# Layer 3 of a four-layer image network: a second pass of one product, one small multiply on another engine, the joining's norms in steps, and its silus beside the chunk's own

## The chip, the cores and the metric

The kernel runs on one core of a Trainium2 chip, as one launch. The time is the device time of that launch in microseconds. The kernel before took 7278.3 us as the median of three runs (7276.84 to 7281.67).

## The reference, cut to what matters

Four layers run one after the other on x of 4 images x 64 channels x 128 x 128, float32. Only the last is touched. It is two selective scans over the same picture and a joining of their results:

```python
xc = silu(causal_conv(x @ in_w)); z = ...
dt, Bm, Cm = split(xc @ xproj_w)            # 16 states
dt = softplus(dt @ dt_w + dt_b)
h  = exp(dt * A) * h + dt * Bm * xc         # the scan, over the positions
y  = (sum over states of h * Cm + xc * D) * silu(z) @ out_w
...
spa = silu(group_norm(scan over all positions of all images)) + x
spe = silu(group_norm(scan over 8 tokens of 8 channels, for each pixel)) + x
w   = softmax(att_w)
out = spa * w[0] + spe * w[1] + x
```

The group norms have 4 groups per image, so neither scan's result can be joined before all of that image has been scanned: group_norm needs the mean and the variance over an image's pixels and 16 channels.

## The kernel before, in words

The network's first three layers end at about 3567 us of the span. Layer 3 works in 142 **chunks**, each of eight **steps**, one step for 16 of the 128 inner channels, with two scans for the halves of the 16 states: 65 chunks of the first scan ("spe", 64 pixels of 8 tokens, all four images side by side on the partitions), one short chunk ("run"), and 19 chunks for each of the four images of the second scan ("spa", 483 positions; the last of an image has 170). The constant ORDER = (0, 2, 4, 6, 1, 3, 5, 7) gives the order of the steps.

What a chunk does, by function and line:

- do_x: three matmuls, then ACT's two silus (xc L1416, zs L1417), then the load of the table set that holds exp and log (L1418).
- do_dt, in nine parts: softplus by relu, abs, exp and log on ACT (L1429 to L1437), summed on PE into a PSUM bank v, copied to dt by ACT (L1445, L1448). Part 8 is dtx = dt * xc: on DVE from v for spa (L1452), on POOL from dt for spe (L1454). dt and dtx are written to DRAM (do_put) and read back spread over partitions (do_copy), through SP's queue.
- do_bc and do_keep: the projections B and C, by PE into PSUM and by ACT into SBUF (L1465).
- for each step: do_exp, two exponentials dA on ACT (L1492) into PSUM; do_dB, dB = dtx * B, on DVE from PSUM (after do_sel on PE) for five of the eight steps (BY_DVE) and on POOL from SBUF for three (L1517); do_scan, two scans on DVE (L1524, L1529); do_hc, h * C on POOL (L1558, for spe two steps at a time).
- do_first, for spe only: the first token needs no scan. Its three parts are bb = B * C of token 0 (L1543), a matmul, and y0 (L1550, DVE).
- do_sums on PE, do_y on DVE (yz, L1600), the output's matmul, ACT copy and store (spa_out, spe_out), and do_stats, DVE's bn_stats (L1665), in every second spa chunk and four of them in every fourth spe chunk.

PSUM has two banks for the name "m", which v, the projections, the first part's matmul, the norms and the joining share, one for "y" and one for "dx". Four more hold dA.

When an image's last spa chunk is done, affine(b) makes the norms' scales and shifts of both scans for that image (L1744 to L1782, with norm_affine, L361 to L377): bn_aggr on DVE, two small matmuls, a square root on ACT and a reciprocal on DVE for each scan, and some twenty one-column or four-column operations on DVE. Then combine joins the image in eight groups of rows: loads (part 0), two silus on ACT with those scales and shifts (L1808, L1809; part 1), sums of three products on PE (parts 2 and 4) and copies by DVE (L1821; parts 3 and 5), and the store. One group goes beside each of the next image's first eight chunks; image 3's have none beside them.

The order of the work on PE, DVE, ACT and POOL is written by hand: scans() collects (8 * chunk + when, function) in a list, sorts it, and issues it in that order; "when" is in steps, so 8 is a chunk. Each engine takes its instructions in the order of this list, and waits at the first one whose data or buffer is not ready. The DMAs on SP's queue are issued by the same calls. In this list affine stands at 15.8 behind its image's last chunk, all of it in one entry. Group i of the joining has its silus at 10.37 + 8 * (i + 1); the do_x of a later chunk stands at 3.1 within a chunk's eight steps.

Of the kernel before, what the change touches and what calls it, by code (L numbers as in the profile page):

```python
# [9 lines left out]
F32 = mybir.dt.float32  # L10
BF16 = mybir.dt.bfloat16
AF = mybir.ActivationFunctionType
ALU = mybir.AluOpType
AX = mybir.AxisListType
# [3 lines left out]
NB, C, N = 4, 64, 128  # L18
# [6 lines left out]
ZC = 33  # L25
# [288 lines left out]
class Net:  # L314
# [1222 lines left out]
    def do_first(self, u, part):  # L1537

        nc = self.nc
        first = lambda t: t[..., 0::8]  # L1540
        if part == 0:
            u["bb"] = self.work.tile([128, 2, CPX], F32, name="bb", bufs=1)
            nc.gpsimd.tensor_tensor(u["bb"], first(u["BC"][0]), first(u["BC"][1]), ALU.mult)  # L1543
        elif part == 1:
            u["g"] = self.ps("m")[:, :CPX]
            for sg in range(2):
                self.mm(u["g"], self.c3["same"], u["bb"][:, sg], sg == 0, sg == 1)
        else:
            u["y0"] = self.work.tile([128, CPX], F32, name="y0", bufs=1)
            nc.vector.tensor_tensor(u["y0"], u["g"], first(u["dtx"]), ALU.mult)  # L1550
# [120 lines left out]
    def scans(self, us):  # L1671
        nc = self.nc
        self.turn, self.o1s = 0, {}
        chunks = GPX // CPX

        todo = []
        steps = [(u, q) for u in us for q in ORDER]
        by_pool = lambda j: ORDER[j % 8] not in BY_DVE
        for ci, u in enumerate(us):
            do = lambda when, f, *a: todo.append((8 * ci + when, len(todo), f, a))  # L1680
            spa = u["spa"]
            if spa:
                do(-22.0, self.spa_load, u)
            else:
                for part, when in enumerate((-2.9, 4.7, 6.42)):
                    do(when, self.do_first, u, part)
                m, i = divmod(u["at"], 4)
                do(-13.0, self.spe_taps, u)
                for g in range(8 if i == 0 else 0):

                    if m:
                        do(-48.0 + 3 * g if m > 1 else -48.0, self.spe_load, m, g)
                for g in range(8 if i == 3 or u["at"] == chunks - 1 else 0):
                    do(12.3 + 3 * g, self.spe_store, m, g)
            do(-12.9, self.do_x, u)
            for part, when in enumerate((-11.65, -11.25, -10.65, -10.05, -9.8, -9.55, -9.3, -9.0, -8.05)):
                do(when, self.do_dt, u, part)
            do(-7.7, self.do_put, u, "dt")
            do(-7.4, self.do_put, u, "dx")
            for k, when in enumerate((-9.07, -8.85, -7.24, -6.59)):  # L1700
                do(when, self.do_bc, u, k)
                do(when + 0.59, self.do_keep, u, k)
            for i, when in enumerate((4.7, 4.74, 5.9, 9.42, 9.74) if u["kind"] != "run" else ()):
                do(when, self.do_sums, u, i)
            if u["kind"] != "run":
                do(10.76, self.do_y, u)
                do(12.2, self.spa_out if spa else self.spe_out, u)
                do(13.64, self.do_stats, u)
        mine = [j for j in range(len(steps)) if not by_pool(j)]
        for j, (u, q) in enumerate(steps):  # L1710
            do = lambda when, f, *a: todo.append((j + when, len(todo), f, a))
            do(-6.0, self.do_copy, u, q, "dt")
            do(-1.56, self.do_exp, u, q, 0)
            do(-1.2, self.do_exp, u, q, 1)
            if by_pool(j):
                do(-6.5, self.do_copy, u, q, "dx")
                do(-4.22, self.do_dB, u, q, nc.gpsimd)
            else:
                do(-1.61, self.do_dB, u, q, nc.vector)
            do(0.1, self.do_scan, u, q, 0)  # L1720
            do(0.5, self.do_scan, u, q, 1)
            if u["kind"] == "run":
                do(0.55, self.keep_run, u, q)
            else:
                do(0.77, self.do_hc, u, q)
        for k, j in enumerate(mine):

            when = mine[k - 1] - 1.28 if k else -2.0
            todo.append((when, len(todo), self.do_sel, steps[j]))
        for ci, u in enumerate(us):  # L1730
            if u["kind"] == "spa" and u["at"][1] == SPC - 1:
                b = u["at"][0]
                do = lambda when, f, *a: todo.append((8 * ci + when, len(todo), f, a))
                do(15.8, self.affine, b)
                for i in range(8):

                    for part, when in enumerate((4.0, 10.37, 16.3, 16.75, 16.8, 17.51)):
                        do(when + 8 * (i + 1), self.combine, b, i, part)
        E = mybir.EngineType
        with self.tc.manual_schedule(engines={E.PE, E.DVE, E.Activation, E.Pool}):  # L1740
            for _, _, f, a in sorted(todo, key=lambda x: x[:2]):
                f(*a)

    def affine(self, b):  # L1744

        nc, c3, sm = self.nc, self.c3, self.small
        mv = sm.tile([128, 2], F32, name="mv0")
        nc.vector.bn_aggr(mv, self.st0.rearrange("p k s -> p (k s)"))
        s0, t0 = self.norm_affine(sm, mv, c3["gm16w"], c3["spa_gn_w"], c3["spa_gn_b"], self.eps)
        mv = sm.tile([128, 4, 2], F32, name="mv1")  # L1750
        for g in range(4):
            nc.vector.bn_aggr(mv[:, g, :], self.st1[:, g].rearrange("p k s -> p (k s)"))
        gm = c3["gme"][:, 128 * b : 128 * b + 128]
        four = lambda name: sm.tile([128, 4], F32, name=name)
        p = self.ps("m")
        self.mm(p[:, 0:4], gm, mv[:, :, 0])
        mean, q, rs = four("mean4"), four("q4"), four("rs4")
        nc.vector.tensor_copy(mean, p[:, 0:4])
        nc.vector.tensor_tensor(q, mv[:, :, 0], mean, ALU.subtract)
        nc.vector.tensor_tensor(q, q, q, ALU.mult)  # L1760
        nc.vector.tensor_tensor(q, q, mv[:, :, 1], ALU.add)
        p = self.ps("m")
        self.mm(p[:, 0:4], gm, q)
        nc.scalar.activation(rs, p[:, 0:4], AF.Sqrt, bias=self.eps)
        nc.vector.reciprocal(rs, rs)
        one = lambda name: sm.tile([128, 1], F32, name=name)
        s1, t1, m = one("s1"), one("t1"), one("m1")
        for of, to in ((rs, s1), (mean, m)):
            nc.vector.tensor_tensor(of, of, c3["goh"], ALU.mult)
            nc.vector.tensor_reduce(to, of, AX.X, ALU.add)  # L1770
        nc.vector.tensor_tensor(s1, s1, c3["spe_gn_w"], ALU.mult)
        nc.vector.tensor_tensor(m, m, s1, ALU.mult)
        nc.vector.tensor_tensor(t1, c3["spe_gn_b"], m, ALU.subtract)
        self.st = (s0, t0, s1, t1)

        k0, k1 = one("k0"), one("k1")
        nc.scalar.activation(k0, t0, AF.Silu)
        nc.scalar.activation(k1, t1, AF.Silu)
        nc.vector.tensor_tensor(k0, k0, c3["att"][:, 0:1], ALU.mult)
        nc.vector.scalar_tensor_tensor(k1, k1, c3["att"][:, 1:2], k0, ALU.mult, ALU.add)  # L1780
        for i in range(2):
            nc.vector.tensor_copy(self.parts(i)[3][:, :, ZC:96], k1.unsqueeze(2).to_broadcast([128, 8, 96 - ZC]))  # L1782

    def parts(self, i):

# [71 lines left out]
```

## Time and profile before

| | us |
|---|---|
| median of three runs | 7278.3 |
| the profiled execution | 7274.59 |
| its span | 7272.8 |
| PE busy, of the span | 6594.7 (91%) |
| DVE busy | 5372.9 (74%) |
| ACT busy | 4715.9 (65%) |
| POOL busy | 3438.8 (47%) |
| mean granted clock of TensorE | 0.952 |

The shares are of the whole span, and the four layers have different loads: PE's 91% are mostly of the first three, POOL's 47% almost all of the last. A share says little of layer 3; stretches of it do, and they are read by the answers to windows. In the groups of instructions each row has: line, engine, operation, tile written <- tiles read, size, count | busy time, mean ns of one | idle time of the engine just before, and what ended it. Busy time counts an instruction from its start to its end, and neighbours overlap a little: a scan of 1145 ns is followed by the next one some 1.11 us after its start.

### The profile page before, as it was taken

To read this page: it belongs to the slowest core of one execution; us is meant where nothing else is said; L and a number is where in the kernel's file an instruction comes from. 1 tells how busy PE (TensorE), PEld (TensorE's weight loads), DVE (VectorE), ACT (ScalarE), POOL (GpSimd) and SP (SyncE) were. 2 spreads that over 40 slices of the span, in tenths; PEclk is the share of its full clock that TensorE was granted. 3 is DMA by queue.
4 is the path that set the end of the run, shared out by engine and by line. 5 is a ranking of instruction groups with operands and counts; after the bars stand their busy time and mean duration, and the time that the engine had idled before them with its cause. 6 is when DMAs were issued, how large, how long until landed. Compare 5 with 4: busy or idle time off the path is not lost. (4 is left out here: it accounts for less than half of the span.)

```text
span 7272.8 us, 106459 instructions
## 1 busy us (share of the span) xinstructions
PE 6594.7 (91%) x39058; PEld 2862.1 (39%) x39058; DVE 5372.9 (74%) x7814; ACT 4715.9 (65%) x7768; POOL 3438.8 (47%) x1571
## 2 busy tenths in 40 slices
PE   8998999989999899988999999999888898898897
PEld 6335563347434563346533323333322332332333
DVE  3665546664565636654499999999999889899896
ACT  2564636653465536652487778777788788888885
POOL 1000000000000000000299999999899789789796
PEclk9998989989999989987999999999999999999998
DMA  3000110002000010002455555555455465554554
GB/s 91 1 1 1 29 47 1 1 1 74 2 1 1 28 47 1 1 1 84 146 149 152 150 151 152 151 151 148 135 159 150 133 175 146 143 170 141 155 165 122
DMA packets 364108, 647.01 MB, mean 89 GB/s; under 512 B 46784, under 2 KB 219584, under 8 KB 362048
## 3 DMA queue, kind: packets, MB, share of 16 engines
q1 hardware_dynamic: 357680, 609.91, 29.8%
q10 hardware_dynamic: 5904, 30.28, 1.2%
q8 instruction: 308, 5.05, 0.3%
q14 instruction: 216, 1.77, 0.1%
HBM read 517.80 MB, written 122.22 MB: 88 GB/s over the span
## 5 line engine op out<-in xcount | busy, mean ns | idle before, releaser
L1558 POOL TENSOR_TENSOR hc<-hd,C 128x910 f32<-128x910 f32 (+3 forms) x868 | 2314.1, 2680 | 250.3 <-DVE hd L1524 189.5
L754 DVE TENSOR_REDUCE nmz<-ps_sp 128x1 f32<-128x320 f32 x2048 | 895.3, 485 | 622.1 <-PE ps_sp L332 612.7
L770 ACT ACTIVATE big<-ps_sp 128x512 f32<-128x512 f32 (+1 forms) x1536 | 830.7, 592 | 719.0 <-PE ps_sp L332 717.7
L1524 DVE TENSOR_TENSOR_SCAN hd<-dA,hd 128x484 f32<-128x484 f32 (+1 forms) x1152 | 1235.3, 1109 | 72.5 <-ACT dA L1492 72.5
L1529 DVE TENSOR_TENSOR_SCAN hd<-dA,hd 128x512 f32<-128x512 f32 (+2 forms) x1120 | 1270.7, 1182 | 3.1 <-ACT dA L1492 3.0
L929 POOL TENSOR_TENSOR aw<-pack_a 128x128 f32<-128x128 f32 x8 | 3.5, 458 | 2185.4 <-PE ps_m L332 2185.4
L1517 POOL TENSOR_TENSOR hd<-s_dx,B 128x1024 f32<-128x1024 f32 (+5 forms) x450 | 960.2, 2135 | 12.0 <-DMA s_dx<-ddx 11.1
L332 PE MATMUL ps_dx<-dtx,c_sel 128*128 128x483 f32 (+3 forms) x1420 | 758.0, 616 | 218.4 <-DVE hd L1517 217.7
L332 PE MATMUL ps_sp<-uT,kT 32*128 32x512 f32 x3072 | 924.1, 649 | 1.4 <-ACT big L770 0.8
L1492 ACT ACTIVATE dA<-s_dt,c_spa_a 128x483 f32<-128x483 f32 (+3 forms) x1232 | 762.4, 640 | 158.1 <-DVE hd L1524 145.5
L1517 DVE TENSOR_TENSOR hd<-ps_dx,B 128x1024 f32<-128x1024 f32 (+5 forms) x750 | 808.4, 1080 | 73.7 <-PE ps_dx L332 72.6
L332 PE MATMUL ps_sp<-kT,qT 32*128 32x320 f32 x4096 | 817.3, 499 | 3.9 <-ACT qT L735 3.3
L1492 ACT ACTIVATE dA<-s_dt,c_spe_a 128x448 f32<-128x448 f32 x1040 | 636.3, 632 | 192.0 <-DVE hd L1529 190.9
L332 PE MATMUL ps_y<-hc,c_sum 128*32 128x455 f32 (+3 forms) x4512 | 603.9, 550 | 44.0 <-POOL hc L1558 44.0
L332 PE MATMUL ps_m<-sr,xht 128*128 128x483 f32 (+4 forms) x1136 | 509.4, 592 | 47.3 <-ACT sr L1436 47.3
L332 PEld LDWEIGHTS ps_dx<-dtx,c_sel 128*128 128x128 f32 x1420 | 225.8, 191 | 691.6 <-DVE hd L1517 289.5
L332 PEld LDWEIGHTS ps_sp<-uT,kT 32*128 32x128 f32 x3072 | 278.7, 185 | 437.5 <-issue 242.2
L332 PE MATMUL ps_o<-big,va 128*32 128x512 f32 (+1 forms) x3072 | 413.1, 610 | 0.0
L332 PE MATMUL ps_s<-pack_a,big 128*64 128x128 f32 (+4 forms) x2832 | 370.4, 305 | 43.5 <-DMA big<-in_x 19.8
L332 PEld LDWEIGHTS ps_sp<-kT,qT 32*128 32x128 f32 x4096 | 358.2, 190 | 57.2 <-issue 36.6
L332 PEld LDWEIGHTS ps_s<-pack_a,big 128*128 128x128 f32 (+2 forms) x2832 | 328.9, 179 | 65.3 <-issue 25.7
L332 PEld LDWEIGHTS ps_m<-sr,xht 128*128 128x128 f32 x1136 | 206.3, 193 | 348.2 <-issue 177.9
(396 smaller groups left out, 9585.7 us busy)
## 6 DMA issues: line engine op xcount, KB each, us to landing
s_dt<-ddt SPq DMA_DIRECT2D x520, 256.0 KB
s_dt<-ddt SPq DMA_DIRECT2D x544, 241.5 KB
s_dx<-ddx SPq DMA_DIRECT2D x195, 256.0 KB
s_dx<-ddx SPq DMA_DIRECT2D x204, 241.5 KB
ddt<-dt SPq DMA_DIRECT2D x65, 256.0 KB
ddx<-dtx SPq DMA_DIRECT2D x65, 256.0 KB
A<-x2s SPq DMA_DIRECT2D x136, 121.2 KB
ddt<-dt SPq DMA_DIRECT2D x68, 241.5 KB
```

Of the source, the lines that this page charges most:

```text
L332: self.nc.tensor.matmul(out, lhsT, rhs, start=start, stop=stop)
L754: nc.vector.tensor_reduce(self.nmz[n % 2][:, j, at : at + 1], p[:, :KEYS], AX.X, ALU.max, negate=True)
L770: nc.scalar.activation(slot(m, 2 * wu + q)[rows], p[rows], AF.Exp)
L929: nc.gpsimd.tensor_tensor(aw[i], k(f"aw{i + 1}"), k("sg"), ALU.mult)
L1492: self.nc.scalar.activation(t(u["dA", q][sg][:, at + u["lo"] : at + u["n"]]), t(u["dt", q]), AF.Exp, scale=a)
L1517: eng.tensor_tensor(v(dB[:, :, x:y]), v(d), v(u["BC"][0][:, :, x:y]), ALU.mult)
L1524: scan(hd[:, :m], dA[:, :m], hd[:, TOK : TOK + m], 0.0, ALU.mult, ALU.add)
L1529: scan(h[:, lo:n], dA[:, at + lo : at + n], dB[:, lo:n], init, ALU.mult, ALU.add)
L1558: mul = lambda to, a, b: self.nc.gpsimd.tensor_tensor(to, a, b, ALU.mult)
```

## The change

Four things are edited. (1) bb of the first scan's first token is computed by DVE in place of POOL. (2) The list of positions for do_dt gets a tenth entry, at -7.45 for the second scan and -8.05 for the first; do_dt itself is as before. The write of dtx to DRAM goes from -7.4 to -7.1 for the second scan. (3) affine is split. The first scan's norms of all four images are made once, in nine steps before image 0's last chunk (spe_affine); the second scan's are made per image, in nine steps (spa_affine) between 13.7 and 20.2. The root and the reciprocal become a log and an exponential of -0.5 times it on ACT, with one Newton step on DVE (rooted). (4) The joining's silus go from 10.37 to 11.095, which within eight steps is directly before the do_x at 3.1.

The diff; the removed body of affine is left out, since it is printed above.

```diff
--- before.py
+++ after.py
@@ -1540,7 +1540,7 @@
         first = lambda t: t[..., 0::8]
         if part == 0:
             u["bb"] = self.work.tile([128, 2, CPX], F32, name="bb", bufs=1)
-            nc.gpsimd.tensor_tensor(u["bb"], first(u["BC"][0]), first(u["BC"][1]), ALU.mult)
+            nc.vector.tensor_tensor(u["bb"], first(u["BC"][0]), first(u["BC"][1]), ALU.mult)
         elif part == 1:
             u["g"] = self.ps("m")[:, :CPX]
             for sg in range(2):
@@ -1693,10 +1693,10 @@
                 for g in range(8 if i == 3 or u["at"] == chunks - 1 else 0):
                     do(12.3 + 3 * g, self.spe_store, m, g)
             do(-12.9, self.do_x, u)
-            for part, when in enumerate((-11.65, -11.25, -10.65, -10.05, -9.8, -9.55, -9.3, -9.0, -8.05)):
+            for part, when in enumerate((-11.65, -11.25, -10.65, -10.05, -9.8, -9.55, -9.3, -9.0, -8.05, -7.45 if spa else -8.05)):
                 do(when, self.do_dt, u, part)
             do(-7.7, self.do_put, u, "dt")
-            do(-7.4, self.do_put, u, "dx")
+            do(-7.1 if spa else -7.4, self.do_put, u, "dx")
             for k, when in enumerate((-9.07, -8.85, -7.24, -6.59)):
                 do(when, self.do_bc, u, k)
                 do(when + 0.59, self.do_keep, u, k)
@@ -1731,55 +1731,115 @@
             if u["kind"] == "spa" and u["at"][1] == SPC - 1:
                 b = u["at"][0]
                 do = lambda when, f, *a: todo.append((8 * ci + when, len(todo), f, a))
-                do(15.8, self.affine, b)
+                for part, when in enumerate((13.7, 14.3, 15.1, 15.7, 16.55, 17.0, 18.0, 19.09, 20.2)):
+                    do(when, self.spa_affine, b, part)
+                for part, when in enumerate((-25.4, -23.4, -22.4, -20.4, -19.4, -18.0, -16.4, -12.91, -11.4) if b == 0 else ()):
+                    do(when, self.spe_affine, part)
                 for i in range(8):
 
-                    for part, when in enumerate((4.0, 10.37, 16.3, 16.75, 16.8, 17.51)):
+                    for part, when in enumerate((4.0, 11.095, 16.3, 16.75, 16.8, 17.51)):
                         do(when + 8 * (i + 1), self.combine, b, i, part)
         E = mybir.EngineType
         with self.tc.manual_schedule(engines={E.PE, E.DVE, E.Activation, E.Pool}):
             for _, _, f, a in sorted(todo, key=lambda x: x[:2]):
                 f(*a)
 
-    def affine(self, b):
...
+    def rooted(self, part, v, r, of=None):
+
+        nc = self.nc
+        if part == 0:
+            nc.vector.tensor_scalar(v, of, 1e-5, None, ALU.add)
+        elif part == 1:
+            nc.scalar.activation(r, v, AF.Ln)
+            nc.scalar.activation(r, r, AF.Exp, scale=-0.5)
+        else:
+            nc.vector.tensor_tensor(v, v, r, ALU.mult)
+            nc.vector.tensor_tensor(v, v, r, ALU.mult)
+            nc.vector.tensor_scalar(v, v, -0.5, 1.5, ALU.mult, ALU.add)
+            nc.vector.tensor_tensor(r, r, v, ALU.mult)
+
+    def spe_affine(self, part):
+
+        nc, c3, st = self.nc, self.c3, self.const
+        keep = lambda name, n: st.tile([128, n], F32, name="sa_" + name)
+        by_b = lambda t: t.rearrange("p (b g) -> p b g", b=NB)
+        each = lambda t: t.unsqueeze(1).to_broadcast([128, NB, 4])
+        if part == 0:
+            self.sa = a = dict(mean=keep("mean", 4 * NB), q=keep("q", 4 * NB), v=keep("v", 4 * NB), k=keep("k", NB))
+            for name in ("s", "t", "m"):
+                a[name] = keep(name, NB)
+            a["mv"] = mv = st.tile([128, 2, 4], F32, name="sa_mv")
+            for g in range(4):
+                nc.vector.bn_aggr(mv[:, :, g], self.st1[:, g].rearrange("p k s -> p (k s)"))
+            return
+        a = self.sa
+        if part in (1, 3):
+            a["p"] = p = self.ps("m")[:, : 4 * NB]
+            for b in range(NB):
+                of = a["mv"][:, 0] if part == 1 else a["q"][:, 4 * b : 4 * b + 4]
+                self.mm(p[:, 4 * b : 4 * b + 4], c3["gme"][:, 128 * b : 128 * b + 128], of)
+        elif part == 2:
+            mean, q = a["mean"], by_b(a["q"])
+            nc.vector.tensor_copy(mean, a["p"])
+            nc.vector.tensor_tensor(q, each(a["mv"][:, 0]), by_b(mean), ALU.subtract)
+            nc.vector.tensor_tensor(q, q, q, ALU.mult)
+            nc.vector.tensor_tensor(q, q, each(a["mv"][:, 1]), ALU.add)
+        elif part in (4, 5):
+            self.rooted(part - 4, a["v"], a["q"], a["p"])
+        elif part == 6:
+            self.rooted(2, a["v"], a["q"])
+            for of, to in (("q", "s"), ("mean", "m")):
+                v = by_b(a[of])
+                nc.vector.tensor_tensor(v, v, each(c3["goh"]), ALU.mult)
+                nc.vector.tensor_reduce(a[to], v, AX.X, ALU.add)
+            of = lambda w: w.to_broadcast([128, NB])
+            nc.vector.tensor_tensor(a["s"], a["s"], of(c3["spe_gn_w"]), ALU.mult)
+            nc.vector.tensor_tensor(a["m"], a["m"], a["s"], ALU.mult)
+            nc.vector.tensor_tensor(a["t"], of(c3["spe_gn_b"]), a["m"], ALU.subtract)
+        elif part == 7:
+            nc.scalar.activation(a["k"], a["t"], AF.Silu)
+        else:
+            nc.vector.tensor_scalar(a["k"], a["k"], c3["att"][:, 1:2], None, ALU.mult)
+
+    def spa_affine(self, b, part):
+
+        nc, c3 = self.nc, self.c3
+        one = lambda name: self.small.tile([128, 1], F32, name=name)
+        if part == 0:
+            self.fa = dict(mv=self.small.tile([128, 2], F32, name="mv0"))
+            nc.vector.bn_aggr(self.fa["mv"], self.st0.rearrange("p k s -> p (k s)"))
+            return
+        a = self.fa
+        mv = a["mv"]
+        if part in (1, 3):
+            a["p"] = self.ps("m")[:, 0:1]
+            self.mm(a["p"], c3["gm16w"], mv[:, 0:1] if part == 1 else a["q"])
+        elif part == 2:
+            a["mean"], a["q"] = one("gn_mean"), one("gn_q")
+            nc.vector.tensor_copy(a["mean"], a["p"])
+            nc.vector.tensor_tensor(a["q"], mv[:, 0:1], a["mean"], ALU.subtract)
+            nc.vector.scalar_tensor_tensor(a["q"], a["q"], a["q"], mv[:, 1:2], ALU.mult, ALU.add)
+        elif part == 4:
+            a["v"], a["s0"] = one("gn_v"), one("gn_s")
+            self.rooted(0, a["v"], a["s0"], a["p"])
+        elif part == 5:
+            self.rooted(1, a["v"], a["s0"])
+        elif part == 6:
+            s0, m, t0 = a["s0"], one("gn_ms"), one("gn_t")
+            a["t0"] = t0
+            self.rooted(2, a["v"], s0)
+            nc.vector.tensor_tensor(s0, s0, c3["spa_gn_w"], ALU.mult)
+            nc.vector.tensor_tensor(m, a["mean"], s0, ALU.mult)
+            nc.vector.tensor_tensor(t0, c3["spa_gn_b"], m, ALU.subtract)
+            self.st = (s0, t0, self.sa["s"][:, b : b + 1], self.sa["t"][:, b : b + 1])
+        elif part == 7:
+            a["k"] = one("k0")
+            nc.scalar.activation(a["k"], a["t0"], AF.Silu)
+        else:
+            k = a["k"]
+            nc.vector.scalar_tensor_tensor(k, k, c3["att"][:, 0:1], self.sa["k"][:, b : b + 1], ALU.mult, ALU.add)
+            for i in range(2):
+                nc.vector.tensor_copy(self.parts(i)[3][:, :, ZC:96], k.unsqueeze(2).to_broadcast([128, 8, 96 - ZC]))
 
     def parts(self, i):
```

More of the change, by code (lines that the diff above doesn't have):

```diff
@@ L1742, in scans @@
                 f(*a)
-    def affine(self, b):
[L1746 to L1782, printed above, removed]
```

## The prediction

> **What bounds the kernel now.** The page comes first. In its 40 slices, of 182 us each, only the last half changes: the diff touches layer 3, from about 3567 us.
>
> ```profile
> DVE  3665546664565636654499999999999889899896
> POOL 1000000000000000000299999999899789789796
> ```
>
> VectorE (DVE) and GpSimd (POOL) are both at nine tenths there, so which of them bounds a chunk must be read by stretch. One answer gives four: two chunks of the first scan (the first with the statistics), image 0's joining norms, and one chunk that carries a joining. The columns are stretch, length, then busy time of PE, weight loads, DVE, ACT, POOL, the granted clock, the DMA share and GB/s.
>
> ```profile
> 4512.00:4537.07 25.07, 22.90 (x89) 7.37 (x88) 25.07 (x27) 20.01 (x32) 24.59 (x10) 1.00 0.56 146
> 4537.10:4562.20 25.10, 23.42 (x90) 7.66 (x89) 24.40 (x24) 19.97 (x32) 25.10 (x10) 1.00 0.49 149
> 5732.86:5746.77 13.91, 3.89 (x12) 2.08 (x10) 7.26 (x29) 6.66 (x11) 4.71 (x3) 0.68 0.16 53
> 5790.30:5818.60 28.30, 25.33 (x92) 9.44 (x92) 25.01 (x29) 24.54 (x38) 23.52 (x12) 0.94 0.63 176
> ```
>
> A plain first-scan chunk is **POOL's**: 25.10 of 25.10. By the starts of the chunks' own silu (L1416), such chunks take 25.07 to 25.10, and every fourth, with four bn_stats, 25.56, all of it DVE's. A plain second-scan chunk, read the same way, takes 23.83 or 24.05 with DVE busy 23.4 or 24.0: it is **DVE's**. A joining chunk takes 28.0 to 28.7 with DVE busy 24.4 to 25.4: about 3.4 us are stalls. In the norms' 13.9 us no scan runs.
>
> **Part 1, first scan.** POOL's groups from 3650 to 5220 us:
>
> ```profile
> L1558 POOL TENSOR_TENSOR hc<-hd,C 128x1792 f32<-128x1792 f32 x250 | 1022.3, 4094 | 9.5 <-PE ps_dx L332 7.0 <-DVE dtx L1452 1.9 <-DVE hd L1529 0.5
> L1517 POOL TENSOR_TENSOR hd<-s_dx,B 128x1024 f32<-128x1024 f32 x187 | 446.9, 2390 | 0.0
> L1454 POOL TENSOR_TENSOR dtx<-dt,xc 128x512 f32<-128x512 f32 x62 | 79.7, 1285 | 0.0
> L1543 POOL TENSOR_TENSOR bb<-B,C 128x128 f32<-128x128 f32 x62 | 42.3, 682 | 0.0
> ```
>
> The work per chunk is 4 hc, 3 dB, one dtx, one bb, with no idle time. From start to start they take 4.07, 2.35, 1.24 and 0.64. The diff takes bb away. But its list for do_dt gains a tenth entry, and do_dt has only `else` behind part 7: the tenth entry computes **dtx a second time**. In the changed program's order POOL issues 130 dtx in place of 65, DVE 154 in place of 77. So POOL's sum rises by 1.24 - 0.64 = 0.60 in 49 chunks: 29.4 us. In the 16 chunks of 25.56 DVE decides: bb there costs it what y0, an op of its size, takes (255 ns busy), 0.2: 3.2. Together **+33**. bb's waits come under part 4.
>
> **Part 2, second scan.** DVE's groups behind 5237 us:
>
> ```profile
> L1452 DVE TENSOR_TENSOR dtx<-ps_m,xc 128x483 f32<-128x483 f32 x68 | 44.9, 661 | 47.1 <-ACT dt L1448 45.9
> L1669 DVE COPY hd<-hd 128x14 f32<-128x14 f32 x8 | 6.1, 765 | 0.3
> L363 DVE TENSOR_TENSOR gn_dv<-mv,gn_mean 128x1 f32<-128x1 f32 x4 | 3.0, 758 | 0.1
> ```
>
> A second dtx costs DVE 661 ns, 0.57 from start to start. Of 76 chunks 27 lie in the stretches of part 3; 49 x 0.57 = 28, less some 3 that DVE's idle time before the first dtx (0.41 per chunk) takes up in uneven chunks: **+25**. The write of dtx to DRAM goes 0.3 step (0.9 us) later, but POOL's first dB that needs it is over 4 steps (12 us) behind: nothing. The bank of v stays held to the second dtx, so later projections (do_bc) and, in joining chunks, the first sums wait on a chain through the one other bank. PE has 2.6 us free in a plain chunk (21.2 of 23.83): I take nothing.
>
> **Part 3, joining.** ACT's loads in the joining chunk at 5790 us:
>
> ```profile
> L1418 ACT ACT_TABLE_LOAD x1 | 1.3, 1283 | 0.0
> L1808 ACT ACT_TABLE_LOAD x1 | 1.3, 1283 | 0.0
> L1492 ACT ACT_TABLE_LOAD x1 | 1.3, 1283 | 0.0
> L1416 ACT ACT_TABLE_LOAD x1 | 1.3, 1283 | 0.0
> ...
> L1808 ACT ACTIVATE xht<-xht,gn_t,gn_s 128x552 f32<-128x552 f32 x1 | 0.8, 848 | 0.0
> L1809 ACT ACTIVATE xht<-xht,t,s 128x520 f32<-128x520 f32 x1 | 0.8, 806 | 0.0
> ```
>
> Two pairs of loads, one pair around each pair of silus. The diff puts the joining's silus directly before the chunk's own: one pair, 2.57 us of ACT less. What was two blocks of 4.2 and 3.8 us, in which no dA is made, is one of 5.4. DVE stalled 2.64 on dA and 0.7 before dtx. The one block, 1.6 longer than a plain chunk's, leaves about 0.8 of stall on dA (0.65 of slack in a plain chunk), and I add 0.4 each for the first sums and yz behind the held bank, plus the second dtx. Period 27.25 in place of 28.28: -1.03 x 24 (three images; the fourth joins in the tail) = -25. The norms go from one block into steps: 13.84 without a scan become 3.65 of DVE work: -10.2 x 3 = -31. Together **-55** (rounded). The low end: chunks at DVE's own 25.3, -47 more.
>
> By "ScalarE: Activation LUTs", What ACT_TABLE_LOAD costs, a switch also drains, 2.66 us in all, so that a pair saved would be 5.3. In the trace the next ACTIVATE starts 0.02 behind a load of 1283 ns; I stay with 2.57, and by the page the joining chunk would be at DVE's own work.
>
> **Part 4, waits for POOL.** The L363 row above has a mean of 758 ns for one column, and tile gn_mean's answer has 158/159/965 for it over 12. DVE and POOL side by side:
>
> ```profile
> 5736.43 0.16 DVE L361 COPY gn_mean<-ps_m 128x1 f32<-128x1 f32 x1 [3.16 <-PE ps_m L332]
> 5736.63 0.96 DVE L363 TENSOR_TENSOR gn_dv<-mv,gn_mean 128x1 f32<-128x1 f32 x1
> 5737.63 0.22 DVE L365 SCALAR_TENSOR_TENSOR gn_q<-gn_dv,mv 128x1 f32<-128x1 f32 x1
> ```
>
> ```profile
> 5733.32 2.09 POOL L1558 TENSOR_TENSOR hc<-hd,C 128x902 f32<-128x902 f32 x1
> 5735.37 2.21 POOL L1517 TENSOR_TENSOR hd<-s_dx,B 128x952 f32<-128x952 f32 x1
> ```
>
> The subtraction, both operands in SBUF, ends as POOL's op ends (5737.58). It does so in all three norms with POOL running, and takes 0.16 in the nine without. keep_run's copy (L1669), SBUF to SBUF, took 3.17 us beside an hc and 0.18 alone. The copy of a PSUM bank at 5736.43 took 0.16 beside the same POOL op. All scans, dB and dtx of DVE have an operand in PSUM; the diff's new steps mostly do not, and they stand among POOL ops of 2.1 to 2.2 us that fill 98% of a second-scan chunk.
>
> "SBUF — State Buffer", Who interferes with whom, states this rule: a DVE instruction with two SBUF operands and a POOL one exclude each other for a whole instruction, at most one does not. It speaks against this change; rows and rule agree, and the rule alone would leave the sum as it is.
>
> Price for one image's steps: q (2 ops), a Newton step with s, m, t (6 tensor_tensor), k with two copies (3). A first wait is on average half a POOL op, 1.1; each next op meets POOL's next op, 2.1, until POOL has used up its backlog, which at 5732.86 lasted 4.7 us. So 3.2 + 4.6 + 4 = 12, x 3 = **+36** (0, if all fall into gaps; 11 waits of 1.5, 50). The first scan's norms run once: 4 bn_aggr of 0.54 and 17 ops of 0.2, 5.6 of DVE's time in chunks that DVE bounds, and 10 of such waits: **+16** (6 to 20).
>
> bb has two SBUF operands as well. It is asked for 2.2 us after a scan; with the second dtx POOL is late enough that a dB (2.35) is then running, so that it waits some 1.4, inside DVE's slack of 25.70 - 24.40. I take nothing, and up to 1.3 in the 16 statistics chunks, +21, for the range.
>
> **Tail.** From image 3's bn_aggr (7208.6) to its first joining silu (7218.2) the norms are a chain of 9.6; without the first scan's part and the loads for roots it is about 5: **-5**.
>
> **Sum.** 33 + 25 - 55 + 36 + 16 - 5 = +50. The profiled execution took 7274.59 (span 7272.8), so 7325; the median of the runs, 7278.3, is 3.7 above it, hence 7328 as a median.
>
> **Rivals.** About 0.2% (14.6 us) is what a measurement of this kernel can tell from no change.
> - *No waits for POOL.* The strewn steps fall where POOL pauses, or hide in DVE's waits. Place: q, Newton, k. Price -46 to -52: 50 - 52 = -2, **7276**, not slower. It decides once waits fall under 37 in all. For it: POOL had 0.5 us free per chunk. Against it: three of three with POOL busy waited. 0.14.
> - *That, and joining chunks at DVE's own work.* -2 - 47 = -49: **7229**. For it: ACT is busy 24.5 of 28.3, less 2.6. Against it: the held bank. 0.08.
> - *bb misses POOL's gap.* If POOL starts its next op first, bb waits for a 4.07 hc: the chunk grows from 25.7 to about 28.7, 65 x 3 = 195: **7523**. Against it: the copy of 3.17 ended at POOL's boundary (5240.7), one sample. 0.10. If only in the statistics chunks, with the upper prices of part 4: 7345 to 7400. 0.18.
> - The forecast, 7293 to 7345: 0.50. *The change doesn't do what it says*: it does, and a second dtx more; the program's order is known.
>
> Faster 0.08, same 0.14, slower 0.78. The range goes from 7265 (most of "no waits") to 7400, and leaves out 0.08 below and 0.10 above.
>
> **What would show it.** L1454 x130 and L1452 x154; plain first-scan chunks at 25.7 with POOL full; plain second-scan chunks at 24.4 to 24.6; joining chunks near 27.2; one-column ops of the new steps with means near 1 to 2 us; bb's mean near 1.5. Wrong, if bb's mean is over 3, or the new steps' ops are at 0.16, or joining chunks come to 25.5.

## The result, and the profile after

The changed kernel takes 7529.7 us as the median of four runs (7526.65 to 7530.98), beside 7280.0 for the kernel before in the same job: ratio 1.0342, 95% interval 1.0325 to 1.036. It is **slower by 250 us**. The forecast was 7328 with a range up to 7400; the time is where the rival "bb misses POOL's gap" had put it, 7523, for a reason that this rival had only half, and in part by luck.

Where the time came in, by the starts of the chunks' silu in the two profiled executions (span 7272.8 before, 7529.2 after):

| stretch | before | after | difference | foreseen |
|---|---|---|---|---|
| layers 0 to 2, up to the first chunk | 3566.3 | 3581.7 | +15.4 | 0 |
| first scan, chunks 3 to 64 | 1562.8 | 1814.2 | +251.4 | +33 |
| second scan away from the joinings | 1095.2 | 1118.5 | +23.3 | +25 |
| chunks 82 and 83, which now hold the first scan's norms | 47.9 | 62.4 | +14.5 | +17, with two dtx |
| three stretches of norms and joining chunks | 795.1 | 751.8 | -43.3 | -19 |
| tail (image 3's norms and joining) | 139.9 | 133.3 | -6.6 | -5 |

(Chunks 0 to 2 add 1.7.) The first row isn't the change: those layers' instructions are the same, and over 14 profiled executions of kernels that differ only in layer 3 the first chunk begins between 3564.9 and 3584.8. Every row but the first scan's is within 25 us of what was foreseen; that one is 218 us above it.

In the page's slices POOL, at nine tenths in the first scan before, is at eight: it no longer bounds the stage. Windows of two first-scan chunks, a plain second-scan chunk and a joining chunk (length, then PE, weight loads, DVE, ACT, POOL, clock, DMA share, GB/s):

```profile
4615.10:4644.95 29.85, 26.14 (x89) 8.44 (x88) 27.45 (x25) 20.32 (x33) 26.76 (x10) 0.89 0.48 131
4644.95:4672.20 27.25, 23.50 (x89) 7.63 (x88) 26.51 (x25) 20.26 (x32) 24.19 (x10) 1.00 0.50 130
5636.90:5661.50 24.60, 21.35 (x76) 6.73 (x76) 24.54 (x26) 20.30 (x34) 23.38 (x12) 1.00 0.53 145
6102.50:6130.00 27.50, 24.02 (x93) 9.22 (x94) 25.14 (x29) 21.64 (x37) 23.49 (x12) 1.00 0.65 180
```

The first scan's chunk varies between 27 and 31, 29.26 on average over chunks 3 to 64, in place of 25.21. The granted clock does not explain it: the chunk at 1.00 is long too. The second scan's is 0.56 longer, the second dtx; the joining chunk is 0.8 shorter. The groups from 3650 to 5220 us say what POOL waits for, and what DVE does:

```profile
L1558 POOL TENSOR_TENSOR hc<-hd,C 128x1792 f32<-128x1792 f32 x216 | 882.3, 4085 | 178.8 <-DVE hd L1529 139.3 <-PE ps_dx L332 24.5 <-PE ps_m L332 15.0
L1454 POOL TENSOR_TENSOR dtx<-dt,xc 128x512 f32<-128x512 f32 x106 | 135.2, 1276 | 4.2
```

```profile
L1543 DVE TENSOR_TENSOR bb<-B,C 128x128 f32<-128x128 f32 x54 | 181.6, 3363 | 43.0 <-PE ps_m L332 43.0
```

Before, hc waited 9.5 us in this stretch, now 178.8, mostly for DVE's scans. And bb, 0.3 us of work on DVE, lasts 3.36 on average, behind 0.8 of idle time that ends with a product of PE. One chunk's timeline of DVE, of POOL and of PE (start, length, then what ran, and in brackets the idle time before with its releaser; the line ps_m<-bb is PE's read of bb, ps_m being one of the two "m" banks, here for g):

```profile
4528.29 2.31 DVE L1529 TENSOR_TENSOR_SCAN hd<-dA,hd 128x512 f32<-128x512 f32 x2
4531.34 3.57 DVE L1543 TENSOR_TENSOR bb<-B,C 128x128 f32<-128x128 f32 x1 [0.74 <-PE ps_m L332]
4534.83 1.22 DVE L1529 TENSOR_TENSOR_SCAN hd<-dA,hd 128x512 f32<-128x512 f32 x1
```

```profile
4528.27 2.35 POOL L1517 TENSOR_TENSOR hd<-s_dx,B 128x1024 f32<-128x1024 f32 x1
4530.59 4.07 POOL L1558 TENSOR_TENSOR hc<-hd,C 128x1792 f32<-128x1792 f32 x1
4534.63 2.51 POOL L1517 TENSOR_TENSOR hd<-s_dx,B 128x1024 f32<-128x1024 f32 x1
```

```profile
4530.65 0.66 PE L332 MATMUL ps_m<-bb,c_same 128*128 128x64 f32 x4
```

DVE's scans end at 4530.60. bb has one buffer, and PE reads the previous chunk's bb until 4531.3, so bb can't start. By then POOL's hc has run for 0.75 us, and bb, with both operands in SBUF, ends just behind it (4534.91 and 4534.66). It is so in every chunk but the first: 64 of the 65 bb start inside an hc and end 0.24 to 0.26 behind its end. The first, at 3597.02, meets no operation of POOL and takes 0.39: two operands in SBUF alone do not make it slow. Had bb been ready at 4530.60, it would have stood at the boundary between dB and hc.

### The profile page after: what moved, and what is told of

The parts are those of the page before. It is cut to its first block, busy times and chain, and to the rows that moved or that the text cites. A ratio compares the mean times of both kernels' runs of the same rounds, so it can differ in the third digit from the quotient of the medians.

```text
span 7529.2 us, 106476 instructions
## 1 busy us (share of the span) xinstructions
PE 6668.4 (89%) x39058; PEld 2870.4 (38%) x39058; DVE 5646.1 (75%) x7925; ACT 4654.2 (62%) x7709; POOL 3492.2 (46%) x1571
## 5 line engine op out<-in xcount | busy, mean ns | idle before, releaser
L332 PE MATMUL ps_dx<-dtx,c_sel 128*128 128x483 f32 (+3 forms) x1420 | 790.8, 640 | 337.6 <-DVE hd L1517 333.0
L1492 ACT ACTIVATE dA<-s_dt,c_spa_a 128x483 f32<-128x483 f32 (+3 forms) x1232 | 759.4, 640 | 178.8 <-DVE hd L1524 160.9
L332 PE MATMUL ps_y<-hc,c_sum 128*32 128x455 f32 (+3 forms) x4512 | 639.4, 581 | 97.3 <-POOL hc L1558 97.3
L332 PE MATMUL ps_m<-sr,xht 128*128 128x483 f32 (+4 forms) x1136 | 524.6, 605 | 60.5 <-ACT sr L1436 60.5
```

What stands on the lines that cost most here:

```text
L332: self.nc.tensor.matmul(out, lhsT, rhs, start=start, stop=stop)
L1492: self.nc.scalar.activation(t(u["dA", q][sg][:, at + u["lo"] : at + u["n"]]), t(u["dt", q]), AF.Exp, scale=a)
```

## The experiments

Two theories were set against each other. **Port** (the "lock theory" of the expectations): bb on DVE waits because both of its operands are in SBUF while POOL's hc runs; where in POOL's work it falls sets the price. **Queue or dtx:** the second dtx on POOL, or bb's place in DVE's order and its wait for PE, makes the chunk long by itself. The kernel before was run beside them in each job: 7284.5, 7284.3, 7280.8 and 7283.8.

**bb back on POOL**, the second dtx kept:

```diff
-            nc.vector.tensor_tensor(u["bb"], first(u["BC"][0]), first(u["BC"][1]), ALU.mult)
+            nc.gpsimd.tensor_tensor(u["bb"], first(u["BC"][0]), first(u["BC"][1]), ALU.mult)
```

> The changed kernel with bb back on POOL; the second dtx stays. Lock theory (bb on DVE, both operands in SBUF, waits to the end of POOL's hc and so makes the first-scan chunk 29.2): the wait is gone, POOL bounds the chunk with 4 hc, 3 dB, 2 dtx and bb, 25.1 + 1.24 = 26.3 to 26.4 us, and the time falls by 62 x 2.8 = 175 to about 7355. Rival (POOL's second dtx makes the chunk long): the chunk stays near 29 and the time near 7520.

Measured: 7374.9 (7373.4 to 7376.7), chunk 26.93. The direction is the port theory's, -155, but the chunk isn't always POOL's 26.3: 25 of the 62 take 27.7 to 28.1, with DVE waiting for the product for dB (132.1 us of idle time before dB between 3650 and 5220 us). More on that below.

**One dtx**, bb left on DVE:

```diff
-            for part, when in enumerate((-11.65, -11.25, -10.65, -10.05, -9.8, -9.55, -9.3, -9.0, -8.05, -7.45 if spa else -8.05)):
+            for part, when in enumerate((-11.65, -11.25, -10.65, -10.05, -9.8, -9.55, -9.3, -9.0, -8.05)):
-            do(-7.1 if spa else -7.4, self.do_put, u, "dx")
+            do(-7.4, self.do_put, u, "dx")
```

> The changed kernel with dtx computed once, as before the change; bb stays on DVE. Lock theory: bb still meets an hc, the first-scan chunk stays between 27.5 and 29.2, and only the second scan's chunks give back 0.56 each (76 of them, 40 us): 7400 to 7490. Rival (the second dtx is what lengthens the first-scan chunk): it falls to 25.0 and the time to about 7225.

Measured: 7395.8 (7392.9 to 7404.0), just under the range; chunk 27.93, bb's mean 2.37. The second dtx isn't the main part of the chunk's length: without it the chunk falls by 1.3 only, and bb still falls into an hc, only later in it.

**Both undone**: the edits of the last two together.

> The changed kernel with dtx computed once and bb on POOL: only the split norms and the joined silus are left. Both theories: first-scan chunk as before (25.07), joining chunks 27.3 - 0.56 = 26.8 in place of 28.3 (24 x -1.5 = -36), norms about -10 each (-30), the first scan's norms +13, tail -5: 7280 - 58 = about 7222. A second rival (the new steps of the norms cost what the old block did): 7245 or more.

Measured: 7219.9 (7203.6 to 7223.6), ratio 0.9906 (0.9892 to 0.9921). What is left of the change, the norms in steps and the joined silus, is **worth 65 us**. Against this kernel bb on DVE alone costs 176, the second dtx alone 155, both together 310.

**One operand of bb in PSUM**: PE copies C's first tokens into the free part of the bank that holds the previous chunk's g; everything else as in the changed kernel.

```diff
-            nc.vector.tensor_tensor(u["bb"], first(u["BC"][0]), first(u["BC"][1]), ALU.mult)
+            tok = self.g_at[:, CPX : 3 * CPX] if self.g_at is not None else self.ps("m")[:, CPX : 3 * CPX]
+            tok = tok.rearrange("p (s x) -> p s x", s=2)
+            self.mm(tok, self.c3["id"], first(u["BC"][1]))
+            nc.vector.tensor_tensor(u["bb"], first(u["BC"][0]), tok, ALU.mult)
         elif part == 1:
-            u["g"] = self.ps("m")[:, :CPX]
+            self.g_at = self.ps("m")
+            u["g"] = self.g_at[:, :CPX]
...
```

> The changed kernel, bb on DVE, but its second operand is first copied by PE into the unused part of the PSUM bank that holds the previous chunk's g, so that DVE reads only one operand from SBUF; the second dtx stays, and PE does one 128-column product more per chunk. Lock theory: bb takes about 0.3 and the chunk falls to 25.7 to 26.0 (POOL's two dtx, no bb): about 7310. Rival (what costs is bb's place in DVE's queue and its wait for PE, not the operands' place): bb and the chunk stay as they are, 7500 or more.

Measured: 7640.6 (7637.5 to 7648.2), a miss. From 3650 to 5220 us:

```profile
L1546 DVE TENSOR_TENSOR bb<-B,ps_m 128x128 f32<-128x128 f32 x50 | 19.3, 386 | 275.5 <-PE ps_m L332 275.5
```

bb itself is 0.39 each time (in 61 chunks beside a running dB of POOL); but DVE waits 5.5 us for the copy, which stands in PE's queue behind sums that wait for an hc. The edit had made a new wait in place of the old one. Mended, with the copy directly behind the previous chunk's g and bb one scan later:

```diff
+            nc.vector.tensor_tensor(u["bb"], first(u["BC"][0]), u["tok"], ALU.mult)
+        elif part == 3:
+            bank = self.g_at if self.g_at is not None else self.ps("m")
+            u["tok"] = bank[:, CPX : 3 * CPX].rearrange("p (s x) -> p s x", s=2)
+            self.mm(u["tok"], self.c3["id"], first(u["BC"][1]))
...
-                for part, when in enumerate((-2.9, 4.7, 6.42)):
+                do(-3.29, self.do_first, u, 3)
+                for part, when in enumerate((-2.45, 4.7, 6.42)):
```

> The changed kernel with bb on DVE and one of its operands in PSUM, as in the run before of that kind, but PE's copy stands directly behind the previous chunk's g and bb one scan later, so that DVE doesn't wait for the copy; the second dtx stays. Lock theory: bb takes 0.39 without any wait for POOL, the first-scan chunk falls from 29.2 to about 26 (POOL's two dtx), and the time to about 7325. Rival (an op more on DVE at this place costs 3 us whatever its operands): 7500 or more.

Measured: 7346.4 (7342.2 to 7350.4), chunk 26.42.

```profile
L1543 DVE TENSOR_TENSOR bb<-B,ps_m 128x128 f32<-128x128 f32 x59 | 21.1, 358 | 0.0
```

```profile
4124.48 0.36 DVE L1543 TENSOR_TENSOR bb<-B,ps_m 128x128 f32<-128x128 f32 x1
```

```profile
4121.54 4.09 POOL L1563 TENSOR_TENSOR hc<-hd,C 128x1792 f32<-128x1792 f32 x1
```

The same multiplication on the same engine, at 0.36 (0.35 to 0.40 over all 65) where it was 3.36. It stands later in the order now, but 63 of the 65 still start inside an hc, mostly with 1.1 us or more of it to go, and don't wait for its end: that both operands are in SBUF is what makes bb wait.

**Two buffers for bb**, on the changed kernel:

```diff
-            u["bb"] = self.work.tile([128, 2, CPX], F32, name="bb", bufs=1)
+            u["bb"] = self.work.tile([128, 2, CPX], F32, name="bb", bufs=2)
```

> The changed kernel with two buffers for bb in place of one, so that bb doesn't wait for PE's read of the previous chunk's bb (0.8 us per chunk in the changed kernel). Lock theory: bb is asked for 0.8 earlier, while the same hc of POOL already runs or just starts, and ends when that hc ends: bb's median grows from 3.6 to about 4.2, the chunk stays near 29 and the time within 15 of 7530. Rival (the wait for PE makes bb miss the gap between POOL's ops): bb comes before the hc, its median falls under 1 and the time to about 7320.

Measured: 7403.9 (7398.5 to 7405.8), bb's median 0.72, its mean from 3650 to 5220 us 0.70. Here the expectation from the port theory **fell**, and the rival was right on bb, though not on the time (7320): one more buffer of 512 bytes per partition takes away 126 us. bb then is asked for while a dB runs (in 63 of the 65 chunks), waits a few tenths for its end, and goes ahead of the hc, which is 4.26 in place of 4.08:

```profile
4140.02 0.72 DVE L1543 TENSOR_TENSOR bb<-B,C 128x128 f32<-128x128 f32 x1
```

```profile
4138.13 2.36 POOL L1517 TENSOR_TENSOR hd<-s_dx,B 128x1024 f32<-128x1024 f32 x1
4140.44 4.26 POOL L1558 TENSOR_TENSOR hc<-hd,C 128x1792 f32<-128x1792 f32 x1
```

So the wait for the port was real, but that it was the wait for an *hc* came from the buffer.

That left open whether the buffer alone decides. **One dtx, two buffers**, on the kernel of the run shown next (7202.5), which has one dtx, bb on POOL and the first scan's norms elsewhere:

```diff
-            u["bb"] = self.work.tile([128, 2, CPX], F32, name="bb", bufs=1)
-            nc.gpsimd.tensor_tensor(u["bb"], first(u["BC"][0]), first(u["BC"][1]), ALU.mult)
+            u["bb"] = self.work.tile([128, 2, CPX], F32, name="bb", bufs=2)
+            nc.vector.tensor_tensor(u["bb"], first(u["BC"][0]), first(u["BC"][1]), ALU.mult)
```

> The kernel with one dtx and the norms in the idle chunks (7202), with one edit: bb on DVE with two buffers. The run with two buffers and two dtx showed bb meeting the end of a dB (0.7) in place of an hc (3.6). Theory that POOL's lag decides where bb falls: without the second dtx POOL is earlier, bb meets an hc just begun, DVE waits 2 to 4 us, the first-scan chunk is 27 or more and the time about 7320 to 7400. Rival (the wait for PE's read alone decided): bb falls into a dB as with two dtx, POOL's chunk loses bb's 0.64, the chunk is 24.5 to 25.0 and the time about 7180 to 7200.

Measured: 7382.6 (7378.2 to 7383.3), chunk 27.92. DVE and POOL in one chunk:

```profile
4121.07 3.40 DVE L1543 TENSOR_TENSOR bb<-B,C 128x128 f32<-128x128 f32 x1
```

```profile
4120.13 4.09 POOL L1558 TENSOR_TENSOR hc<-hd,C 128x1792 f32<-128x1792 f32 x1
4124.17 2.53 POOL L1517 TENSOR_TENSOR hd<-s_dx,B 128x1024 f32<-128x1024 f32 x1
```

No wait for PE any more, and bb still waits 3: without the second dtx POOL is earlier, and the hc began 0.94 before bb. Both conditions are needed: bb early enough, and POOL late enough.

**The first scan's norms in the idle chunks**, on the kernel with both undone:

```diff
-                for part, when in enumerate((-25.4, -23.4, -22.4, -20.4, -19.4, -18.0, -16.4, -12.91, -11.4) if b == 0 else ()):
+                for part, when in enumerate((-146.0, -145.4, -144.8, -144.2, -143.6, -142.8, -141.8, -140.91, -139.5) if b == 0 else ()):
```

> One dtx and bb on POOL, and the first scan's norms moved from beside image 0's last full chunks to the chunks just behind the first scan, where POOL is busy 10 us of 24. If the price of these steps (two chunks of 62.6 in place of 47.9) is DVE's waits for POOL and its full queue there: those two chunks go back to 24 each and the steps cost 0 to 4 at their new place, 7220 - 13 = about 7207. Rival (the steps cost their chain of PE, ACT and DVE wherever they stand): 7220.

Measured: 7202.5 (7197.3 to 7206.4), ratio 0.9887 (0.9872 to 0.9902): the fastest of all, 82 us under the kernel before in its job. Chunks 82 and 83 are back at 47.9, and chunk 67 grew by 5.8, so the move is worth some 9 by the chunks' starts; the rest of the 17 between the two medians lies within the spread of the runs.

**The silus apart again**, on the kernel with both undone:

```diff
-                    for part, when in enumerate((4.0, 11.095, 16.3, 16.75, 16.8, 17.51)):
+                    for part, when in enumerate((4.0, 10.37, 16.3, 16.75, 16.8, 17.51)):
```

> One dtx and bb on POOL, and the joining's silus back at 10.37, away from the chunk's own: only the norms in steps are left of the change. If the joined silus make the joining chunk 26.2 in place of 28.3: 24 x 2.1 = 50 come back, 7220 + 50 = about 7270. Rival (the steps of the norms brought most of the gain): 7235 or less.

Measured: 7263.5 (7255.4 to 7270.3), joining chunks back at 28.36 on average of seven for each image. So the joined silus are worth 44 of the 65, and the norms in steps, with the first scan's at their bad place, the other 21.

**bb on DVE with a PSUM operand and one dtx**, on the kernel with the norms in the idle chunks; the copy and bb's place are as in the mended run:

```diff
-            nc.gpsimd.tensor_tensor(u["bb"], first(u["BC"][0]), first(u["BC"][1]), ALU.mult)
+            nc.vector.tensor_tensor(u["bb"], first(u["BC"][0]), u["tok"], ALU.mult)
```

> The kernel with one dtx and the norms in the idle chunks (7202), with one edit: bb on DVE with one operand copied to PSUM by PE. Lock theory: bb takes 0.36 wherever it falls, POOL's chunk loses 0.64, DVE's 24.4 gains 0.3: plain chunks 24.7, those with bn_stats 25.9, so 49 x -0.35 + 16 x 0.3 = -12, about 7190. Rival (PE's copy and the held bank cost the first-scan chunk what the move gains): 7202 or more.

Measured: 7213.5 (7207.5 to 7215.2), 11 more than 7202.5. bb takes 0.37, in 61 chunks beside a running dB of POOL, and POOL has its 0.64 less (24.4), yet a plain chunk stays at 25.07, with 0.4 of DVE's time waiting for the product for dB, and one with statistics grows to 25.87. Moving bb to DVE in this form doesn't pay even without its waits; why DVE waits there is open.

**The rest of the second dtx.** With bb's wait gone the chunk was 26.42 or, with two buffers, 27.31, and POOL's work is 25.7. DVE, in the run with two buffers, waits for the product for dB (114.5 us from 3650 to 5220 us) as in the run with bb on POOL; PE and DVE there:

```profile
4144.76 1.22 PE L332 MATMUL ps_y<-hc,c_sum 128*32 128x448 f32 x4 [2.22 <-POOL hc L1558]
4145.91 2.08 PE L332 MATMUL ps_dx<-dtx,c_sel 128*128 128x512 f32 x2
```

```profile
4148.02 1.22 DVE L1517 TENSOR_TENSOR hd<-ps_dx,B 128x1024 f32<-128x1024 f32 x1 [2.78 <-PE ps_dx L332]
```

POOL, late by the second dtx, gives hc late; PE stands at the sum over it, and the product for DVE's dB is queued behind that sum. PE has little room to catch up: contrary to what was said of its 91% ahead of the prediction, it is about as busy in layer 3 as before it (3275 us from 3567 us on, 3320 up to there), and 22.9 to 23.4 of a first-scan chunk's 25.1. The edit puts the sum behind the product:

```diff
-            for i, when in enumerate((4.7, 4.74, 5.9, 9.42, 9.74) if u["kind"] != "run" else ()):
+            for i, when in enumerate((4.7, 5.8 if not spa else 4.74, 5.9, 9.42, 9.74) if u["kind"] != "run" else ()):
```

> The changed kernel with two buffers for bb (7404), with one edit: PE's first sums over hc in a first-scan chunk go from 4.74 to 5.8, behind the product for dB at 5.72. If what is left of the chunk's length (27.3 where POOL's work is 25.7) is PE standing at sums whose hc POOL has not finished, so that the product for DVE's dB behind them comes late: the chunk falls to 25.8 to 26.3 and the time by 62 x 1.2 to about 7330. Rival (POOL's second dtx delays DVE's scans by another way, through its own dB or dt): no change, 7404.

Measured on the kernel with two buffers: 7382.1 (7366.9 to 7409.6), inconclusive: in chunks 20 to 29 the length is 24.8 to 27.1 (26.0 on average), but in chunks 30 to 38 it is 28.0 to 30.4, with bb in the hc again, and it changes back and forth. bb's place isn't stable, and it hid the answer. So the same edit on the kernel with bb's operand in PSUM, where bb doesn't wait for the port:

> The kernel with bb on DVE and its operand in PSUM and two dtx (7346), in which no wait for POOL's port remains, with one edit: PE's first sums in a first-scan chunk go from 4.74 to 5.8, behind the product for dB. If the second dtx costs its POOL time and, on top, late sums that hold PE's queue (DVE idle 1.76 per chunk for the product): the chunk falls from 26.42 to POOL's 25.7 and the time by 62 x 0.7 = 43 to about 7303. Rival (PE's queue isn't what holds DVE): 7346.

Measured: 7297.2 (7285.9 to 7309.3) in place of 7346.4, the chunk at 25.75 on average and a plain one at POOL's length:

```profile
4100.00:4125.70 25.70, 23.77 (x94) 7.94 (x95) 24.64 (x25) 20.02 (x33) 25.62 (x10) 1.00 0.66 150
```

## Why the prediction was wrong, point by point

- **The step that failed** is the last of part 4, on bb: "a dB (2.35) is then running, so that it waits some 1.4, inside DVE's slack ... I take nothing". It named the rule of the wait rightly and placed POOL about rightly (with two buffers bb did meet a dB, with 0.47 of it left in place of 1.4), but it put the wait for PE at nothing and took bb to be ready when DVE comes to it, 2.2 us after a scan. It was not: bb has one buffer, and the last reader of the previous one is a product of PE 0.4 step earlier in the order. In the kernel before this cost nothing, because bb stood in POOL's queue, which was late: there PE's read ended some 4.6 us before the next bb began. On DVE that wait of 0.8 moved bb from the end of a dB into the next hc: a step priced at 0 (up to 21) cost, by the run with two buffers, 126, and bb on DVE with both waits 176 to 183 (against bb on POOL, with one dtx; against bb with a PSUM operand, with two).
- The rival on bb had the price nearly right (3 us in each of 65 chunks; the first scan came out 218 above the forecast, 3.5 for each of 62) and its reason wrong: POOL did start the hc first, but not in a contest at the boundary; bb wasn't there yet. That the total fell on its 7523 is partly luck: the norms and joinings gave 24 more than foreseen, and the layers in front, which the change doesn't touch, took 15 more. In all timelines shown where bb waits, it ends at a boundary, and POOL's next op is lengthened (2.51 and 2.53 in place of 2.35, 4.26 in place of 4.08).
- **The second dtx in the first scan** was mis-sized. POOL's own 1.24 is right: with nothing else in the way the chunk is 25.7, as the sum said. But what POOL's lateness does to others was left out: with bb on POOL the first scan's 62 chunks are 107 longer with two dtx than with one, where 1.24 each makes 77; the rest is PE's queue behind the late sums. That was shown by moving them in the kernel with bb's operand in PSUM (26.42 to 25.75); for bb on POOL it is carried over, not shown.
- The second scan's second dtx was right: 0.56 to 0.57 per plain chunk, +23.3 for +25. The joining period came to 27.44 for 27.25. The runs split it as foreseen: 28.3 with the silus apart and 26.3 joined, both with one dtx; the second dtx and, as was assumed, the held bank add 1.2.
- The norms' waits had the right mechanism and too large a size for the second scan: 12 per image foreseen, 5.8 measured in four of eleven instructions. Nor did these 5.8 lengthen the stretch: by the starts of the silus the four chunks from an image's last one on took 110.9 and, with the silus apart and one dtx, take 100.3, 102.7 and 100.9, 9.6 less on average, where the sum had -10.2 without any wait. That is why the norms and joinings together gave 24 more than foreseen. Not every op met a running op of POOL's. DVE's Newton step for image 0:

```profile
6036.73 0.16 DVE L1757 TENSOR_TENSOR gn_v<-gn_v,gn_s 128x1 f32<-128x1 f32 x1
6036.92 0.15 DVE L1758 TENSOR_SCALAR gn_v<-gn_v 128x1 f32<-128x1 f32 x1
6037.11 1.82 DVE L1759 TENSOR_TENSOR gn_s<-gn_s,gn_v 128x1 f32<-128x1 f32 x1
6038.97 2.14 DVE L1831 TENSOR_TENSOR gn_s<-gn_s,c_spa_gn_w 128x1 f32<-128x1 f32 x1
6041.14 0.16 DVE L1832 TENSOR_TENSOR gn_ms<-gn_mean,gn_s 128x1 f32<-128x1 f32 x1
```

  Two of these waited. POOL began its hc only at 6036.79, when the first had begun, and had run dry when the last came (idle from 6041.09 to 6043.77). The chunk that holds most of the norms fell from 41.8 to 32.5. The first scan's norms cost 14.5 with the second dtx of two chunks in it, and 14.7 in the run with one dtx and bb on POOL, for 16, and the tail gave 6.6 for 5.

## What to carry to other kernels

When an operation moves to another engine, list what it waits for in the old queue at no cost because that queue was late: a single buffer whose last reader comes just before is such a wait, and it counts on the new engine. A short instruction that has to share a port costs not its own time but what is left of the other engine's instruction at the moment it becomes ready, so price it by that moment and not by an average; if the moment is within a microsecond of a boundary, both sides have to be forecast. And work added to an engine that bounds a stage is paid again by the queues that wait for its results in order: look at what stands behind the wait.

## What the runs showed of the hardware that was not expected

- One small multiplication, 0.36 us with an operand in PSUM, lasted up to 3.94 us in the changed kernel with both in SBUF beside POOL. "SBUF — State Buffer", Who interferes with whom, has this rule, and that the loser blocks fully; the runs agree, in that 64 of 65 bb ended just behind the end of the hc.
- An instruction with a single SBUF operand waited too: of the first scan's norms, a tensor_scalar over 16 columns took 2.13 beside a dB of POOL's, and 0.15 with one column, at 6036.92 beside an hc. The same page says that copies and tensor_scalar can take the shared port in their two-port modes, when their operands meet certain conditions; that the one column did not meet them is argued, not shown. The prediction's short form of the rule, that an instruction with at most one SBUF operand does not wait, left this out, although its own copy of 3.17 us (L1669) had only one.

```profile
5929.10 2.13 DVE L1758 TENSOR_SCALAR sa_v<-sa_v 128x16 f32<-128x16 f32 x1
```

```profile
5928.99 2.21 POOL L1517 TENSOR_TENSOR hd<-s_dx,B 128x952 f32<-128x952 f32 x1
```

- In the run with two buffers and the later sums the chunk has two regimes in one execution, 24.8 to 27.1 with bb beside a dB (chunks 20 to 29) and 28.0 to 30.4 with bb beside an hc (30 to 38), and the run's times range over 43 us. What makes it go from one to the other isn't shown.
